# Grouping a layer's column-tiled products in the order of TensorE, and loading a layer's constants through GpSimd

## The chip, the cores and the metric

The kernel runs on one NeuronCore of one Trainium2 chip. The number that counts is the device time of one execution in microseconds; before the change it is 3792.88 us, the median of three runs that lie between 3792.59 and 3792.96 us. TensorE (PE) does the matrix products, VectorE (DVE), ScalarE (ACT) and GpSimd (POOL) the elementwise work, and SyncE (SP) mostly issues transfers (DMAs). Each engine carries out its own queue in order and waits for others by semaphores.

## The reference

32 graphs of 512 nodes, with 256 features per node (x) and a 512x512 0/1 matrix (adj), go through four layers. Each layer is x + layer(relu(layernorm(x))).

- Layer 0 is graph attention with 4 heads of 64 features: h = x W, scores leaky_relu(src_i + dst_j) where adj is set, softmax over j, product with h, elu.
- Layer 1 is graph attention with one head and 256 features, with the softmax over i in place of j.
- Layer 2 has scores leaky_relu((h * a_0) h^T); where adj is 1 they are used, the rest is masked; softmax over j, product with h.
- Layer 3 is a transformer block: queries, keys and values (Wqkv), 8 heads of 32 features, masked softmax, output product (Wo), layernorm, a hidden layer of 1024 features with relu (W1, W2), layernorm.

```
scores = einsum('bhqd,bhkd->bhqk', q * scale, k)
attn   = softmax(where(allowed, scores, -inf))
ctx    = einsum('bhqk,bhkd->bhqd', attn, v)
x      = layernorm(x + ctx @ Wo.T + bo)
x      = layernorm(x + relu(x @ W1.T + b1) @ W2.T + b2)
```

## The kernel before

`quick_path` handles one graph at a time with 128 partitions by NT = 4 tiles of 128 nodes and KD = 2 tiles of 128 features. Everything is float32; the masks are bfloat16. An f32 product appears as two MATMUL instructions in the profile, so the counts there are twice those in the code (transposes by an identity matrix count once).

**Jobs and places.** The layers don't issue instructions; they hand jobs to a `Plan` (`plan.dve`, `plan.act`, `plan.dma`, `plan.matmuls`). The job number `at` of graph `number` gets the place `number * ROUND + PLACES[at]`, with ROUND = 100000 and one table of 509 numbers, `PLACES`, that is the same for all graphs. `carry_out` sorts all jobs by place and issues them in that order, chaining the jobs of one engine to each other, so that each engine's queue is exactly that order. The last number of the table is 506629: about five graphs are in work at a time, each in another stage, and after the first graphs every stretch of 100000 places, a round, holds one whole graph's worth of jobs from several graphs. A matmul job is a list of products that stand together in PE's queue. Costs such as `takes`, `fixed`, `FULL`, `HALF` were for the making of the table and do nothing at run time.

**Buffers.** A `Kind` is a tag with a number of slots: two PSUM slots `ps_a`, two `ps_b`, one `ps_ct`, one `ps_to`; in SBUF six `p`, two `p3`, eight `st` and so on.

**Products.** PE's jobs are of three kinds. Most use the whole array (128 rows by 128 columns). In layer 3, `ps_s`, the scores of four heads, are four products with 32 contracted rows each, one per quarter of the rows (32*128 in the profile). `ps_ct`, values times probabilities, and `ps_to`, the sums of the probabilities by a matrix of ones, are four products with 32 output columns each, one per quarter of the columns (128*32). Per graph there are 8 jobs of each of the three, in the loop over `g` (2 groups of heads) and `j` (4 tiles of keys); each is 8 MATMULs. `ps_ct` and `ps_to` are separate jobs with separate places, so other products can stand between them.

```
plan.matmuls(0.93, *((ps_ct[at], v[...], p[:, r], ...) for r, at in enumerate(heads)))
plan.matmuls(0.98, *((ps_to[at], ones, p[:, r], ...) for r, at in enumerate(heads)))
```

Between the scores and these, ACT takes the exponential (two instructions into `p3`) and DVE multiplies by the mask m3.

**Layer 1's column sums.** For each j, DVE makes p (`scalar_tensor_tensor` of rows and mc), then ACT copies p into mc only to accumulate its sum (`activation`, AF.Copy, accum_out=rt[:, 3]), which adds an accumulator read; then DVE takes the reciprocal and ACT scales wh with it.

**The start.** Before the plan, the preamble loads the weights and constants of all layers through ACT's queue (`weight_of`, `rows_of`, `cols_of`), 6 for layers 0 to 2 and 15 for layer 3, in program order ahead of ACT's first computation. DVE folds the attention vectors into w0_t and w1_t (lines 396 to 405), scales bqk_c (407), and a small product ps_bv (line 414) folds the values' bias into bo_r. SP loads adj and x of graph 0 (places 0 and 38476). Layer 0 needs the transposed mask mT: four DMA transposes on SP, then the source scores go through DRAM to all partitions (rows_d, rows).

**Helpers' lines.** Line 208 stands for all DVE and ACT jobs, 242 for products, 240 for transposes, 229 for SP's DMAs.

## Time and profile before

| | us |
|---|---|
| median of three runs | 3792.88 |
| the profiled execution | 3795.71 |
| its span, first to last instruction | 3794.3 |
| PE busy | 3675.7 (97%) |
| DVE busy | 2726.3 (72%) |
| ACT busy | 1899.4 (50%) |
| POOL busy | 0.9 |
| mean granted TensorE clock | 0.981 of full |

The profile gives busy time by engine, the span in 40 slices, waits by releaser, groups of instructions by shape, and a timeline in which neighbouring instructions of one group are merged (start, length, xcount). A product's length is modelled and overlaps the next one's; the time that a group holds PE is the distance from its start to the next start.

### The profile page before, as it was taken

What the parts mean: (1) busy time and instruction counts of PE and PEld (TensorE: products, weight loads), DVE (VectorE), ACT (ScalarE), POOL (GpSimd) and SP (SyncE); (2) the same over time, 40 slices, a digit from 0 to 9 for tenths busy, and PEclk for the clock granted to TensorE, in tenths of its full rate; (3) what the DMA queues carried; (4) which work ended last, traced back from release to release, by engine and by line L of the source; (5) the groups of instructions that cost most, each with busy time, mean ns of one, the idle gap of its engine ahead of it and who ended that gap; (6) DMA issues with size and microseconds to landing.
All of it is one profiled execution on the core that took longest, in us unless ns stands there. A gap on an engine that the chain in (4) does not pass through costs nothing.

```text
span 3794.3 us, 51918 instructions
## 1 busy us (share of the span) xinstructions
PE 3675.7 (97%) x19974; PEld 2333.5 (62%) x19974; DVE 2726.3 (72%) x6139; ACT 1899.4 (50%) x3649; POOL 0.9 (0%) x10
## 2 busy tenths in 40 slices
PE   4799999999999999999999999999999999999996
PEld 4656666665666665666666666656666656566543
DVE  4677777787777787777787777777777778777653
ACT  1255544555544555545555554455555455554543
POOL 0000000000000000000000000000000000000000
PEclk7799999999999999999999999999999999999998
DMA  3211111111101111101111101111111111110000
GB/s 115 61 43 43 35 31 43 48 43 43 44 22 44 47 43 43 45 21 48 43 43 49 40 21 48 43 43 48 42 29 37 43 48 44 43 34 15 15 9 10
DMA packets 156239, 152.74 MB, mean 40 GB/s; under 512 B 90064, under 2 KB 126416, under 8 KB 151888
## 3 DMA queue, kind: packets, MB, share of 16 engines
q1 hardware_dynamic: 149632, 144.35, 12.4%
q10 hardware_dynamic: 6352, 4.99, 0.4%
q8 instruction: 160, 2.62, 0.3%
q14 instruction: 95, 0.78, 0.1%
HBM read 114.57 MB, written 17.96 MB: 35 GB/s over the span
## 4 chain that ended last, share of the span: by engine, by line
PE 95%; DVE 2%; DMA 1%; ACT 1%; issue 0%; ACTq 0%; DVEq 0%
PE ps_o L242 25%; PE ps_f L242 24%; PE ps_s L242 7%; PE ps_wh L242 6%; PE ps_ct L242 6%; PE ps_to L242 6%; PE ps_qk L242 6%; PE ps_t L240 4%; PE ps_e L242 4%; PE ps_v L242 3%; PE ps_wo L242 3%; DVE p L208 1%; PE ps_y L240 1%; DMA rows<-rows_d 0%; DMA ff_t<-in_L_gnn_W_dram 0%; PE ps_sp L240 0%
## 5 line engine op out<-in xcount | busy, mean ns | idle before, releaser
L242 PEld LDWEIGHTS ps_o<-wh,p 128*128 128x128 f32 x5120 | 694.8, 196 | 171.5 <-issue 93.6
L242 PE MATMUL ps_o<-wh,p 128*128 128x65 f32 (+1 forms) x5120 | 749.7, 301 | 21.6 <-DVE p L208 21.5
L208 DVE TENSOR_TENSOR p<-p,m 128x2048 f32<-128x2048 f32 x256 | 585.1, 2286 | 47.2 <-ACT p L208 47.2
L208 ACT ACTIVATE p<-ps_s 128x1024 f32<-128x1024 f32 x512 | 500.7, 1021 | 177.5 <-PE ps_s L242 177.5
L242 PE MATMUL ps_f<-tT,ff_t 128*128 128x512 f32 x1024 | 464.4, 602 | 1.7 <-ACT tT L208 1.7
L242 PE MATMUL ps_f<-ff_t,f 128*128 128x256 f32 x2048 | 459.2, 380 | 0.0
L242 PEld LDWEIGHTS ps_f<-ff_t,f 128*128 128x128 f32 x2048 | 384.5, 190 | 64.7 <-issue 16.7
L208 DVE SCALAR_TENSOR_TENSOR p<-rows,rt,mT 128x512 f32<-128x512 f32 x512 | 366.9, 738 | 14.0 <-DMA rows<-rows_d 14.0
L242 PEld LDWEIGHTS ps_f<-tT,ff_t 128*128 128x128 f32 x1024 | 191.5, 192 | 219.2 <-issue 171.8
L208 ACT ACTIVATE f<-ps_f,ff1b_c 128x512 f32<-128x512 f32 x256 | 165.6, 685 | 311.4 <-PE ps_f L242 311.4
L208 ACT ACTIVATE h<-x,shift,rstd 128x256 f32<-128x256 f32 x512 | 272.3, 590 | 86.8 <-PE ps_o L242 46.7
L242 PE MATMUL ps_s<-qk 32*128 32x512 f32 x2048 | 296.2, 641 | 1.2 <-ACT p L208 1.1
L242 PE MATMUL ps_ct<-p,v 128*32 128x512 f32 x2048 | 272.8, 605 | 5.0 <-DVE p L208 4.9
L242 PE MATMUL ps_to<-p,ones 128*32 128x512 f32 x2048 | 266.3, 603 | 3.0 <-DVE p L208 3.0
L242 PE MATMUL ps_o<-h,p 128*128 128x257 f32 x1024 | 246.6, 388 | 0.4 <-DVE p L208 0.4
L242 PE MATMUL ps_qk<-h3T,wqkv_t 128*128 128x512 f32 x512 | 233.1, 599 | 1.5 <-ACT h3T L208 1.5
L242 PEld LDWEIGHTS ps_o<-h,p 128*128 128x128 f32 x1024 | 186.6, 190 | 77.5 <-DVE inv L208 26.0
L208 DVE BATCH_NORM_STATS2 st<-x 128x6 f32<-128x256 f32 x512 | 204.5, 415 | 2.2
L208 DVE COPY spr<-ps_sp 8x128 f32<-8x128 f32 (+1 forms) x64 | 17.8, 278 | 258.8 <-PE ps_sp L240 258.8
L208 ACT ACTIVATE mc<-p 128x512 f32<-128x512 f32 x128 | 80.5, 629 | 209.8 <-DVE p L208 209.8
L240 PEld LDWEIGHTS ps_t<-ident,h 128*128 128x128 f32 x1024 | 125.3, 146 | 95.7 <-issue 27.2
L242 PEld LDWEIGHTS ps_s<-qk 32*128 32x128 f32 x2048 | 82.0, 183 | 163.9 <-issue 50.2
(120 smaller groups left out, 4488.6 us busy)
## 6 DMA issues: line engine op xcount, KB each, us to landing
adj<-in_adj_dram SPq DMA_DIRECT2D x32, 1024.0 KB
rows<-rows_d SPq DMA_DIRECT2D x32, 1024.0 KB
x<-in_x_dram SPq DMA_DIRECT2D x32, 512.0 KB
rows<-rows_d SPq DMA_DIRECT2D x32, 512.0 KB
out_dram<-y SPq DMA_DIRECT2D x32, 512.0 KB
inv<-in_d SPq DMA_DIRECT2D x32, 256.0 KB
ff_t<-in_L_gnn_W_dram ACTq DMA_DIRECT2D x2, 1024.0 KB
mT<-m SPq DMA_TRANSPOSE x128
```

Of the source, the lines that this page charges most:

```text
L208: return [getattr(unit, method)(*map(real, args), **{k: real(v) for k, v in kw.items()})]
L240: made.append(self.nc.tensor.transpose(*map(real, c)))
L242: made.append(self.nc.tensor.matmul(*map(real, c[:3]), start=c[3], stop=c[4]))
```

## The change

1. `ps_ct` and `ps_to` of one (g, j) become one matmul job: four value products, then four sums.
2. In layer 1 ACT's copy for the sum is removed; DVE's `scalar_tensor_tensor` that makes p gets accum_out=rt[:, 3].
3. Layer 3's 15 loads leave ACT's queue. They become POOL DMAs, planned just behind graph 0's loads of x and adj (place 19808), each waiting until graph 0's x has landed. The folding that needs them (bqk_c, ps_bv, bo_r, b2_r, b1_r: six DVE jobs and one PE job) becomes jobs at place 150000, in all queues between graph 0's layer 0 and graph 1's.
4. A new table of 497 numbers (12 jobs fewer), ending at 491710. x now comes before adj. `st` has 7 slots in place of 8; ff2b_r gets its own buffer; ACT's table is loaded by another call at the same spot. The `takes` numbers change too, which does nothing at run time.

```
-                plan.matmuls(
-                    0.93,
+                plan.matmuls(
+                    1.764,
                     *(
                         (ps_ct[at], v[:, j, g * P + r * HD : g * P + (r + 1) * HD], p[:, r], j == 0, j == NT - 1)
                         for r, at in enumerate(heads)
                     ),
+                    *((ps_to[at], ones, p[:, r], j == 0, j == NT - 1) for r, at in enumerate(heads)),
                 )
-                plan.matmuls(0.98, *((ps_to[at], ones, p[:, r], j == 0, j == NT - 1) for r, at in enumerate(heads)))
...
             plan.dve(
-                "scalar_tensor_tensor", p[:, j], rows[:, 0], rt[:, 2, j : j + 1], mc, OP.max, OP.mult, fixed=0.21
+                "scalar_tensor_tensor", p[:, j], rows[:, 0], rt[:, 2, j : j + 1], mc, OP.max, OP.mult,
+                accum_out=rt[:, 3, j : j + 1], fixed=0.21,
             )
-            plan.act("activation", mc, p[:, j], AF.Copy, accum_out=rt[:, 3, j : j + 1], fixed=0.4)
...
+    def load(self, tile, source, behind):
+        wait = mybir.DependencyInfo(mybir.DependencyClass.Sync, mybir.DependencyReason.DATA)
+        def call():
+            made = self.nc.gpsimd.dma_start(tile, source)
+            self.tc.add_manual_dep(made.ins, behind().made.name, wait, reason="in turn")
+            return [made]
+        return self.put("POOL", 1.0, 0.1, [], [], call)
...
-    wqkv_t = weight_of(nc, const, wqkvT, "wqkv_t")
+    wqkv_t = weight_of(nc, const, wqkvT, "wqkv_t", load=later)
...
+    plan.aside(max(PLACES[:2]) + 1)
+    for tile_, source in late:
+        plan.load(tile_, source, lambda: first)
+    plan.aside(ROUND + ROUND // 2)
+    plan.dve("tensor_scalar_mul", bqk_c[:, :KD], bqk_c[:, :KD], SCALE)
+    bv_w, ps = new("p", "bv_w", [P, N]), new("ps_a", "ps_bv", [P, N])
+    for k in range(KD):
+        plan.dve("tensor_copy", bv_w[:, cut(k, P)], bv_c[:, k : k + 1].to_broadcast([P, P]))
+    plan.matmuls(HALF, *((ps[:, :D], bv_w[:, cut(k, P)], wo_t[:, k], k == 0, k == KD - 1) for k in range(KD)))
+    plan.dve("tensor_add", bo_r, ps[:, :D], bo_r)
+    plan.dve("tensor_scalar_add", b2_r, b2_r, -2.0)
+    plan.dve("tensor_add", b1_r, b1_r, ff2b_r)
...
 PLACES = [
-    0, 38476, 64990, 78041, 65188, 65188, 65188, 72767, 130287, 255105, 157691, 242001, 270048, 276929, 44320,
...
+    19807, 0, 43241, 57619, 64598, 73580, 81389, 88138, 134062, 235662, 143142, 287307, 285553, 232853, 15635,
...
```

Sorted by place, the two tables put PE's jobs of one round in these orders. Written from the first `ps_s` of a graph to the products that follow its attention; names as in the profile, the number is the count of jobs, c+t is the new joint job, and ps_o is of layer 0 (o0), 1 (o1) or 2 (o2).

```
before: s, 2 o1, s, 2 wh, to, ct, s, 2 wh, ct, 2 wh, to, s, sp, to, 8 t, ct, s, 3 e, to, e,
        ct, s, ct, 3 y, 2 e, to, s, 2 y, 2 e, ct, to, 2 o0, s, 2 o0, 2 o2, y, ct, o2, 2 to,
        2 o2, ct, 3 o0, then t, wo, wh, o0, f1, f2, qk, v
after:  s, 2 o1, s, 2 wh, c+t, s, 4 wh, c+t, s, c+t, sp, 8 t, s, 4 e, c+t, s, 3 y, 2 e, c+t,
        s, e, 2 y, e, c+t, s, y, 4 o0, 2 o2, c+t, c+t, 2 o2, then wo, o0, t, wh, f1, f2, v, qk
```

On SP, graph 0's order is x, adj, mT, mT, rows_d, mT, rows, mT (before: adj, x, four mT, rows_d, rows), and likewise for every graph.

## The prediction

> **What bounds the kernel now.** I read the page's busy shares first, then the waits of PE, then busy time by stretch, then one round of the timeline.

> ```profile
> PE 3675.7 (97%) x19974; PEld 2333.5 (62%) x19974; DVE 2726.3 (72%) x6139; ACT 1899.4 (50%) x3649; POOL 0.9 (0%) x10
> ```

> ```profile
> 0.00:100.00 100.00, 46.67 (x185) 39.91 (x185) 41.28 (x109) 15.45 (x38) 0.86 (x10) 0.73 0.41 128
> 100.00:200.00 100.00, 80.66 (x426) 67.26 (x425) 61.77 (x171) 31.04 (x79) 0.00 (x0) 0.79 0.14 39
> 300.00:400.00 100.00, 100.00 (x582) 64.76 (x580) 79.23 (x175) 53.10 (x103) 0.00 (x0) 1.00 0.15 46
> 3400.00:3500.00 100.00, 100.00 (x548) 64.25 (x547) 71.20 (x161) 48.42 (x94) 0.00 (x0) 1.00 0.10 30
> 3700.00:3794.00 94.00, 64.47 (x306) 30.35 (x306) 37.12 (x55) 28.74 (x41) 0.00 (x0) 0.84 0.03 10
> ```

> The columns are PE, PEld, DVE, ACT, POOL, then clock and DMA. From 300 to 3500 us PE is busy without a break, and the list of waits for that stretch is empty. Only the ends, where few graphs are in work, have idle PE. So DVE, ACT and DMA work is free in the middle, unless an order makes PE wait for it; what counts is how long PE's own products take.

> They don't take the same time everywhere. One round in PE's timeline:

> ```profile
> 2017.57 5.31 PE L242 MATMUL ps_qk<-h3T,wqkv_t 128*128 128x512 f32 x12
> ...
> 2028.77 1.05 PE L242 MATMUL ps_wh<-w_t,h0T 128*128 128x264 f32 x4
> 2029.65 3.62 PE L242 MATMUL ps_o<-wh,p 128*128 128x256 f32 x16
> ...
> 2038.99 1.16 PE L242 MATMUL ps_wh<-w_t,h0T 128*128 128x264 f32 x4
> 2040.08 1.07 PE L242 MATMUL ps_to<-p,ones 128*32 128x512 f32 x8
> 2040.96 1.04 PE L242 MATMUL ps_ct<-p,v 128*32 128x512 f32 x8
> 2041.94 1.14 PE L242 MATMUL ps_s<-qk 32*128 32x512 f32 x8
> ...
> 2044.09 1.06 PE L242 MATMUL ps_ct<-p,v 128*32 128x512 f32 x8
> 2045.09 1.16 PE L242 MATMUL ps_wh<-w_t,h0T 128*128 128x264 f32 x4
> 2046.18 1.07 PE L242 MATMUL ps_to<-p,ones 128*32 128x512 f32 x8
> ...
> 2130.59 0.59 PE L242 MATMUL ps_qk<-h3T,wqkv_t 128*128 128x512 f32 x1
> ```

> From ps_qk to the next graph's is 113.02 us: the round. From start to next start, eight ps_to followed by ps_ct, the same shape of tile, hold PE 0.88 us, but eight ps_ct followed by ps_wh 1.00. Four ps_wh hold it 0.88 between full products, but 1.09 between ps_s and ps_to. No engine is waited for there: changing the tile shape costs PE about 0.1 us at each edge. That is the term the change acts on.

> **The change part by part.**

> *The joint job and the new order.* In a round of the old order the column-tiled products (ct, to) are left 13 times for another shape (8 for full products, 5 for ps_s) and follow one of their own 3 times. In the new order they are left 7 times and follow their own 9 times. ps_s is entered and left as often as before. Three rows price that.
> - Leaving: 0.996 against 0.883 us (0.972 where the one before was column-tiled too). Old, by place: 15.53 us for the 16 jobs. New: 7 x 0.972 + 9 x 0.883 = 14.75. Gain 0.78.
> - Entering from a full product: 12 times before, 6 after, 0.093 each (1.09 above is 0.88 plus one such edge plus the next). Gain 0.56.
> - The first full product behind another shape: 0.05 (small ones) to 0.105 us (wh, e) dearer; 15 such before, 9 after, but two dear ps_e are new among them. Item by item, gain 0.21.

> Sum 1.54 us a round: 113.03 becomes 111.49. The same listing over all 32 graphs, the incomplete rounds at both ends included, gives 3611.7 us of full-clock PE work before and 3564.8 after: 46.9 less, near 28 full rounds (322 to 3487 us) x 1.54 = 43.1 and 3.8 at the ends. The remaining 182.6 us of the span are the start, the end and the slow clock there.

> That holds if PE waits as little as now. DVE's work per round (2726 / 32 = 85 us) and ACT's (59) stay well below 111. But individual products stand close to their inputs. A sums job of the old order and the mask product that it uses:

> ```profile
> 2045.84 2.29 DVE L208 TENSOR_TENSOR p<-p,m 128x2048 f32<-128x2048 f32 x1 [0.35 <-ACT p L208]
> ...
> 2048.45 0.16 PEld L242 LDWEIGHTS ps_to<-p,ones 128*32 128x32 f32 x8
> ```

> Its data is there at 2048.13, 0.32 us ahead. For each product I added up, in either order, the PE time since the product that its inputs descend from, less the durations of the DVE and ACT steps between: its room if nothing queues in front of those steps. The pair shown has 1.84 us by this count, so queues took 1.52; at another one (mask product 2061.52 + 2.28, ct at 2064.22) they took 1.2 of 1.64. In the new order no room is negative. The smallest are ps_f1 behind the transposes of n (0.88 us for a chain of 0.84), ps_e behind its transposes (1.45 for 1.30), and ct behind ps_s 1.30, 1.55 and 2.22 us. The old order, with 0.05 and 0.3 as its smallest, doesn't wait. I take no wait; if queues take 1.52 of the 1.30, the wait is 0.2 a round, and two or three such places make the 0.5 us a round (31 rounds: 16 us) that the range takes in.

> *The sum on DVE.* ACT loses 4 x (0.629 + 0.189) us a round, hidden: ACT is idle 50%. On DVE, p takes

> ```profile
> L208 DVE SCALAR_TENSOR_TENSOR p<-rows,rt,mc 128x512 f32<-128x512 f32 x128 | 94.3, 738 | 0.0
> L208 ACT ACTIVATION_READ_ACCUMULATOR mc<-p 128x1 f32 x128 | 24.2, 189 | 0.0
> ```

> No accumulating DVE instruction is in the trace. Lower bound 0, upper bound an extra read of 0.189 us plus the whole p again, 0.74: 0 to 3.7 us a round. I take the read alone, as ACT pays only that beside its pass: 0.76 us of DVE. PE hides it (85 of 111 us busy); without that cover the loss is 24 us in all. The chain to ps_o of layer 1 gets shorter by ACT's 0.63.

> [...]

> *The start.* ACT's first computation stands behind the 15 issues:

> ```profile
> 16.19 0.23 DVE L208 BATCH_NORM_AGGREGATE mv<-st 128x2 f32<-128x6 f32 x2
> 22.50 0.59 ACTq L37 DMA_DIRECT2D ff2b_r<-in_L_gnn_b_dram  x1
> 23.20 0.30 ACT L208 ACTIVATE rstd<-mv,eps 128x4 f32<-128x4 f32 x1 [21.17 <-DMA g_r<-in_L_gnn_ln_g_dram]
> ```

> Its input is ready at 16.42, so the first chain can move 6.8 us forward; x first in SP's queue may add to that, up to 11 in all, when DVE's folding of w0 and w1 (ends 19.0) becomes the last. Two things give some back. SP now has rows_d, which waits for the scores, ahead of two of the four mT transposes (1.3 us each, 5.23 for four): one more transpose is in the path, 1.3 us. And the folding at place 150000 stands between graph 0's layer 0 and graph 1's first transposes: 0.17 + 2 x 0.36 on DVE, 2.08 for ps_bv on PE, about 3 us, with graph 1's copy of h0T queued behind it on DVE. Net -2.5 us, from -11 to +8.

> *The loads on POOL.* The folding is reached about when graph 0's layer 0 ends, near 80 us (x is written at 79.4 to 80.6). ACT issues the 15 in 7.41 to 23.09, 15.7 us. No POOL DMA is in the trace. Bounds: as on ACT, or each as long as ACT's longest, 2.40: 36 us. From x's landing at 12 at the latest they'd be issued by 28 to 48, and landed some 11 us later (the longest DMA in the chain is 11.3). Both are before 80, so I take 0; each microsecond past 80 would stop DVE's queue and with it PE, 1 for 1. They also share the DMA engines with mT and rows of graph 0: 1 MB of rows took 41.88 - 37.01 = 4.9 us; up to 5 us more, in the range.

> [...]

> *The end.* The last graph's reciprocals now wait for sums that stand behind the values' products: +0.9 us.

> Sum: -46.9 - 2.5 + 0.9 = -48.5. The profiled execution of 3795.71 would become 3747.2, and the median, which lies 2.8 below it, 3744.4; I say 3744.

> **The rivals.**

> *A. DVE's accumulation makes it slower.* If p costs the full 0.93 us more and PE waits for all of it, that is 3.7 us a round over 31 rounds: +115, with -48.5 about 3859. It decides from 1.6 us of wait a round up (48.5 / 31). For it: DVE's multiplies end just ahead of their products. Against it: DVE idles 26 us a round, and layer 1's chain loses an ACT step.

> *B. The order is too tight.* PE waits 0.5 to 1.2 us a round for ACT or DVE: 16 to 37 us lost, 3760 to 3781. For it: the 0.04 us of room of ps_f1 and queues I didn't cost. Against: the old order is as tight and PE doesn't wait.

> *C. The loads come late.* At 5 us each on POOL they'd end near 12 + 75 + 11 = 98: +18, 3762. Slower than before only from 7 us each (48.5 us late: 128.5 - 23, by 15).

> *D. It changes nothing.* It would need the shape costs to be something else, say a slow weight load, that moves with the jobs. The 0.88 and 1.00 us of the same eight products speak against it: 3790.

> **How the numbers follow.** Forecast 0.74, 3728 to 3762: the start's -11 to +8, waits up to 0.3 us a round, and some 7 us less for the idle time of the first three rounds, whose order changes too and which I priced only at its two ends. B 0.11; C 0.04; A 0.09, of which 0.07 end above and 0.01 level; D 0.02. The range takes in the forecast, C and half of B: 3728 to 3772. A difference under 0.2% (7.6 us) can't be told from no change here. Faster: forecast, B, C and the rest of A, 0.90. Same 0.03, slower 0.07.

> **What would show it.** A round of 111.5 us from ps_qk to ps_qk with no PE wait between 300 and 3500; c+t jobs of 1.86 us (0.88 + 0.98) where another shape follows. The first rstd near 16 us. p's mean in layer 1 at 0.74 and a read below 0.2. POOL's last DMA before 60 us. A round near 113 without waits would refute the shape costs; a wait of PE by DVE p or ACT tT would be rival A or B; a gap of PE near 75 us that ends by a DMA would be C.

## The result, and the profile after

The changed kernel takes 3757.43 us (median of 4, 3756.09 to 3758.1) against 3792.92 for the kernel before, run beside it: ratio 0.9905, 95% interval [0.9888, 0.9923]. That is 35.5 us less; 48.5 were forecast. The profiled span went from 3794.25 to 3756.16 us, 38.1 less, and the comparison below goes by these two.

The page of the changed kernel, busy time of PE and the rest:

```profile
PE 3635.0 (97%) x19974; PEld 2366.4 (63%) x19974; DVE 2732.6 (73%) x6267; ACT 1803.8 (48%) x3393; POOL 11.1 (0%) x25
```

The same stretches as before, with the same columns (PE, PEld, DVE, ACT, POOL, granted clock, DMA share, GB/s):

```profile
0.00:100.00 100.00, 48.29 (x194) 41.72 (x195) 42.77 (x110) 15.27 (x38) 11.12 (x25) 0.70 0.44 129
100.00:200.00 100.00, 77.59 (x309) 64.78 (x309) 49.67 (x137) 23.16 (x56) 0.00 (x0) 0.62 0.13 37
300.00:400.00 100.00, 100.00 (x543) 61.60 (x543) 75.28 (x169) 52.97 (x99) 0.00 (x0) 1.00 0.16 41
3400.00:3500.00 100.00, 98.56 (x547) 62.28 (x540) 69.09 (x157) 48.77 (x85) 0.00 (x0) 1.00 0.04 12
3700.00:3756.00 56.00, 34.96 (x117) 21.87 (x115) 14.77 (x42) 11.66 (x22) 0.00 (x0) 0.82 0.03 11
```

The middle is again full: the list of PE's waits between 340 and 3450 us is empty. The second row is the surprise. From 100 to 200 us PE did less than before (309 matrix instructions where there were 426) at a granted clock of 0.62 where it had been 0.79.

One round of PE's timeline, from the first ps_v to the next graph's, with one of the joint units:

```profile
2006.62 0.59 PE L259 MATMUL ps_v<-wqkv_t,h3T 128*128 128x256 f32 x2
...
2029.14 1.07 PE L259 MATMUL ps_ct<-p,v 128*32 128x512 f32 x8
2030.03 1.04 PE L259 MATMUL ps_to<-p,ones 128*32 128x512 f32 x8
2031.00 1.14 PE L259 MATMUL ps_s<-qk 32*128 32x512 f32 x8
...
2118.00 0.59 PE L259 MATMUL ps_v<-wqkv_t,h3T 128*128 128x256 f32 x2
```

The round is 111.38 us, and 111.37 or 111.38 almost throughout (before: 113.02 or 113.03). In the unit shown, ps_ct followed by ps_to holds PE 0.89 us from start to start, and ps_to followed by ps_s 0.97.

Layer 1's p with its accumulation, and the read that it costs (count, total us, mean ns, idle before):

```profile
L214 DVE SCALAR_TENSOR_TENSOR p<-rows,rt,mc 128x512 f32<-128x512 f32 x128 | 93.5, 749 | 2.3
L214 DVE DVE_READ_ACCUMULATOR p<-rows,rt,mc 128x1 f32 x128 | 10.6, 83 | 0.0
```

The start, with the first and the last of POOL's loads:

```profile
5.90 0.85 POOL L243 DMA_DIRECT2D wqkv_t<-in_L_gnn_Wqkv_dram  x1 [4.46 <-DMA x<-in_x_dram]
7.61 0.30 ACT L214 ACTIVATE rstd<-mv,eps 128x4 f32<-128x4 f32 x1 [5.57 <-DVE mv L214]
24.24 0.55 POOL L243 DMA_DIRECT2D ff2b_r<-in_L_gnn_b_dram  x1
```

**Where the 38.1 us came from.** I cut both spans where graph 1 and graph 29 begin layer 3 (its first ps_qk or ps_v) and split PE's time in each end into three: its work at full clock, what a clock of 0.5 adds to it (half of PE's busy time in the stretches where the granted clock is 0.5), and idle time. The 28 rounds between have no idle time and no slow clock. (What the half clock adds is therefore an estimate from the busy time; layer 0's four ps_o ahead of a ps_wh hold PE 1.60 us at 120.6 us of the changed kernel, where the clock is 0.50, and 0.84 at 2078.6, where it is 1.00.)

| us | before | after | difference |
|---|---|---|---|
| head, to graph 1's layer 3 | 322.12 | 335.96 | +13.8 |
| - work at full clock | 209.4 | 205.9 | -3.5 |
| - added by the half clock | 35.7 | 51.4 | +15.7 |
| - idle | 77.0 | 78.7 | +1.7 |
| 28 rounds | 3164.8 | 3118.6 | -46.2 |
| tail, from graph 29's layer 3 | 307.3 | 301.7 | -5.7 |
| - work at full clock | 253.7 | 250.0 | -3.7 |
| - added by the half clock | 12.0 | 9.2 | -2.9 |
| - idle | 41.6 | 42.5 | +0.8 |

PE's work fell by 53.4 us, more than the 46.9 of the forecast. What was lost is in the head: it should have become shorter and became 13.8 us longer, by about as much as the half clock added. The clock's record begins only at 32.2 us before and at 22.0 after; ahead of that it counts as full, though eight ps_t take 2.01 us at 14.8 us of the changed kernel and 1.04 in the middle. PE's busy time there is 7.3 and 6.8 us, so the differences in the table would change by some 0.3 us.

When graph 0 and graph 1 pass through the head, the difference after minus before develops like this: first ps_t -12.2 us, graph 0's first ps_o -9.2, graph 1's first ps_o -3.5, graph 0's first ps_e +10.4, its layer 3 +19.4. The early start was there; 8.7 of its 12.2 us were used up by graph 1's first ps_o (at 96 us), and the rest by graph 0's layer 1 (its ps_sp at 131.3 us, 124.9 before).

Two views of 3.4 us stretches show the clock in that place, with PE's busy time in the second column and the clock in the third from the end. Before:

```profile
114.20:117.60 3.40, 3.40 (x13) 2.73 (x14) 2.46 (x7) 0.59 (x1) 0.00 (x0) 0.50 0.00 0
117.60:121.00 3.40, 3.40 (x28) 3.26 (x27) 1.78 (x4) 0.75 (x2) 0.00 (x0) 1.00 0.00 0
```

After:

```profile
117.20:120.70 3.50, 3.50 (x14) 3.13 (x13) 0.27 (x1) 0.37 (x1) 0.00 (x0) 0.50 0.00 0
120.70:124.10 3.40, 3.40 (x16) 3.21 (x15) 0.00 (x0) 0.37 (x1) 0.00 (x0) 0.50 0.00 0
124.10:127.50 3.40, 3.40 (x16) 3.21 (x16) 0.75 (x3) 0.00 (x0) 0.00 (x0) 0.50 0.00 0
...
151.80:155.20 3.40, 3.30 (x8) 2.71 (x9) 0.46 (x3) 2.77 (x4) 0.00 (x0) 0.51 0.22 43
155.20:158.60 3.40, 3.40 (x18) 2.95 (x17) 0.42 (x1) 0.72 (x3) 0.00 (x0) 1.00 0.00 0
```

In both, PE has something to do for all but 0.1 us of these stretches. Before, the clock comes back at 117.6; after, it stays at 0.5 until 155.2, though PE is busy from 117.2 to 127.5 without a break. Half clock lasted 102 us in the head before, with 71 us of PE's busy time in it, and 147 us after, with 103. The last section comes back to this busy PE at half clock.

### The profile page after: what moved, and what is told of

Its sections match the earlier page's. It is cut to its first block, busy times and chain, and to the rows that moved or that the text cites. A ratio compares the mean times of both kernels' runs of the same rounds, so it can differ in the third digit from the quotient of the medians.

```text
span 3756.2 us, 51774 instructions
## 1 busy us (share of the span) xinstructions
PE 3635.0 (97%) x19974; PEld 2366.4 (63%) x19974; DVE 2732.6 (73%) x6267; ACT 1803.8 (48%) x3393; POOL 11.1 (0%) x25
## 3 DMA queue, kind: packets, MB, share of 16 engines
q1 hardware_dynamic: 149632, 144.35, 13.8%
q10 hardware_dynamic: 1248, 1.05, 0.1%
## 4 chain that ended last, share of the span: by engine, by line
PE 95%; DVE 3%; ACT 1%; DMA 1%; issue 1%; SPq 0%; ACTq 0%; DVEq 0%
PE ps_o L259 25%; PE ps_f L259 24%; PE ps_s L259 7%; PE ps_ct L259 7%; PE ps_wh L259 6%; PE ps_qk L259 6%; PE ps_to L259 6%; PE ps_e L259 4%; PE ps_t L257 4%; PE ps_v L259 3%; PE ps_wo L259 3%; DVE p L214 1%; PE ps_y L257 1%; DVE st L214 0%; DMA mT<-m 0%
## 5 line engine op out<-in xcount | busy, mean ns | idle before, releaser
L259 PE MATMUL ps_o<-wh,p 128*128 128x65 f32 (+1 forms) x5120 | 750.5, 303 | 30.2 <-DVE p L214 24.6
L259 PEld LDWEIGHTS ps_o<-wh,p 128*128 128x128 f32 x5120 | 705.6, 200 | 102.7 <-issue 60.5
L259 PE MATMUL ps_o<-h,p 128*128 128x257 f32 x1024 | 239.0, 385 | 0.0
L214 DVE BATCH_NORM_STATS2 st<-x 128x6 f32<-128x256 f32 x512 | 195.6, 415 | 6.8 <-DMA x<-in_x_dram 4.7
L214 ACT ACTIVATE rstd<-mv,eps 128x4 f32<-128x4 f32 x192 | 56.4, 294 | 298.6 <-DVE mv L214 286.0
L257 PE MATMUL ps_t<-ident,h 128*128 128x128 f32 x1024 | 172.6, 281 | 25.0 <-ACT h L214 17.6
L259 PEld LDWEIGHTS ps_s<-qk 32*128 32x128 f32 x2048 | 81.3, 182 | 164.6 <-ACT y L214 78.0
```

What stands on the lines that cost most here:

```text
L214: return [getattr(unit, method)(*map(real, args), **{k: real(v) for k, v in kw.items()})]
L257: made.append(self.nc.tensor.transpose(*map(real, c)))
L259: made.append(self.nc.tensor.matmul(*map(real, c[:3]), start=c[3], stop=c[4]))
```

## The experiments

Theory T: the head lost its time to the granted clock, which the new order lets fall earlier and come back later. Rival L: the head is a chain of DVE and ACT steps and PE's clock matters little. Rival F: the loads through GpSimd and the folding between the graphs hold it up. For the rounds: theory S, the price of changing the tile shape, against O, something else in the new order.

### The unit alone, in the old order (joint_only)

```diff
                 plan.matmuls(
-                    0.93,
+                    1.764,
                     *((ps_ct[at], v[...], p[:, r], j == 0, j == NT - 1) for r, at in enumerate(heads)),
+                    *((ps_to[at], ones, p[:, r], j == 0, j == NT - 1) for r, at in enumerate(heads)),
                 )
-                plan.matmuls(0.98, *((ps_to[at], ones, p[:, r], j == 0, j == NT - 1) for r, at in enumerate(heads)))
 PLACES: the old list; a unit takes the later of its two old places (two units: that of ps_to)
```

> The old kernel, in which each values' job and its sums' job are put as one unit of eight products, at the later of their two old places (at the sums' place where a reader of both stands before the values' place); all else, the order of everything else included, is the old kernel's. Theory S (what a round gained is the price of changing the tile shape): the listing of this order has 9 column-tiled units followed by their own kind, 4 that go to ps_s and 3 to full products (old: 3, 6 and 8), and by the prediction's rows a round of 111.64 us, 1.4 less than 113.03; the whole 42 us less, about 3751, with the head unchanged, first layer 3 of graph 1 at 320 to 323 us. Rival O (the new order of the other work made the gain): the round stays at 112.8 to 113.1 and the time above 3785.

Measured: 3793.77 us, ratio 0.9999 [0.9989, 1.0008], and a round of 113.03, as in the kernel before to a hundredth. By the time alone rival O has won. The list of PE's waits between 500 and 3400 us says otherwise (us in total, times, longest):

```profile
PE ps_t L240 <- DVE mv L208: 11.6, 25, 0.5
PE ps_o L242 <- DVE p L208: 9.6, 25, 0.4
```

The kernel before has no wait there. This one waits twice in each round, 0.85 us, and PE's busy time in a round is 112.18 where it was 113.03: the unit saves 0.85 us of work, and 0.85 us of new waits take it back. The same rows that promised 1.39 us a round were therefore too dear by some 0.5 in this order. The timeline shows the first wait:

```profile
2047.94 0.28 PE L240 MATMUL ps_sp<-ident,rt 128*16 128x128 f32 x1
...
2048.26 0.28 DVE L208 COPY spr<-ps_sp 16x128 f32<-16x128 f32 x1
2048.46 0.16 DVE L208 BATCH_NORM_AGGREGATE mv<-st 128x2 f32<-128x6 f32 x1
...
2048.68 1.06 PE L240 MATMUL ps_t<-ident,h 128*128 128x128 f32 x8 [0.46 <-DVE mv L208]
```

And the kernel before at the same place:

```profile
2048.24 0.28 PE L240 MATMUL ps_sp<-ident,rt 128*16 128x128 f32 x1
2048.45 1.07 PE L242 MATMUL ps_to<-p,ones 128*32 128x512 f32 x8
2049.45 1.09 PE L240 MATMUL ps_t<-ident,h 128*128 128x128 f32 x8
```

In the old order a job of eight ps_to (1.00 us from start to next start) stood between ps_sp and these transposes, and covered DVE's two steps. Joined to its ps_ct it stands elsewhere. The other wait is the same with a ps_ct between the last ps_y and ps_o2. That the two sums agree to a hundredth of a us I take for chance: each wait is set by the DVE steps beside it.

### The unit, with the two covers back (joint_cover)

```diff
 PLACES of joint_only, but the units 337/338 and 369/370 take the earlier of their two old places
-    399642 -> 396426 (ps_ct, ps_to between ps_sp and ps_t)
+    428748 -> 425188 (ps_ct, ps_to between ps_y and ps_o2)
```

> Like joint_only, but two of the eight units stand at the earlier of their two old places: so a column-tiled unit lies again between ps_sp and the transposes behind it, and another between the last ps_y and ps_o2, the two places where joint_only made PE wait 0.5 and 0.4 us a round. If joint_only's gain was eaten by these two uncovered DVE steps alone: no PE wait in the middle, and by the prediction's rows (8 units followed by their own kind, 3 by ps_s, 5 by full products) a round of 112.07 us, 0.95 less than before, about 3764. If the rows are wrong and the unit gains nothing in itself: 112.8 to 113.1 again, 3790 or more.

Measured: 3771.78 us, ratio 0.9941 [0.9925, 0.9958]; a round of 112.21, no PE wait between 500 and 3400 us. So the unit is worth 0.82 us a round by itself (forecast from the rows: 0.95), and S stands: with the old order otherwise kept, nothing but the changes of shape has gone. The other half of the changed kernel's 1.65 us needs the new places.

### The loads back on ACT's queue (loads_back)

```diff
-    wqkv_t = weight_of(nc, const, wqkvT, "wqkv_t", load=later)
+    wqkv_t = weight_of(nc, const, wqkvT, "wqkv_t")
...
-    plan.aside(max(PLACES[:2]) + 1)
-    for tile_, source in late:
-        plan.load(tile_, source, lambda: first)
-    plan.aside(ROUND + ROUND // 2)
-    plan.dve("tensor_scalar_mul", bqk_c[:, :KD], bqk_c[:, :KD], SCALE)
...
+    nc.vector.tensor_scalar_mul(bqk_c[:, :KD], bqk_c[:, :KD], SCALE)
...
```

> The changed kernel with layer 3's constants loaded on ACT's queue again and folded ahead of the first graph, as before; order, units and the sum on DVE stay new. If the loads through GpSimd, with the folding between the graphs, give what graph 1's first products showed (3.5 us earlier than before): 3 to 8 us slower than the changed kernel, 3760 to 3765. Rival F (the folding inside the order is what held the head up, 13.8 us): 3743 to 3750. In both cases the round stays at 111.37.

Measured: 3761.86 us (0.9919 [0.9902, 0.9935]), round 111.38, layer 3 of graph 1 at 338.9 us: 4.4 us slower than the changed kernel, 3.0 of it in the head. The loads help; F falls. Its start is that of the kernel before (graph 0's first ps_o at 45.6 us, 44.0 before), and its head is 16.8 us longer, 1.6 of them there already at that ps_o. The other 15 or so are left for the new order; head_old_a and head_old_b, below, test that.

### Idle products in the waits (after_warm, before_warm)

```diff
+    warm = new("ps_ct", "warm", [P, N])
+    for place, count in ((80715, 11), (132759, 3), (140000, 8), (180715, 10), (240000, 6), (254300, 3), (257400, 3)):
+        plan.aside(place)
+        for _ in range(count):
+            plan.matmuls(FULL, (warm, ident, wqkv_t[:, 0, :N], True, True))
```

In the kernel before: `((95439, 10), (152147, 7), (195439, 10), (252147, 11))`, and the method `aside` with it.

> The changed kernel with 44 idle products (identity by 512 columns of a weight, into the values' PSUM tile, read by nobody) where PE waits in the first 155 us: 11 behind the first ps_sp, 3 and 8 inside and behind graph 0's layer 0, 10 behind graph 1's ps_sp, 6, 3 and 3 behind graph 1's layer 0. Theory T (the head is long because TensorE's granted clock stays at half for 147 us, with 103 us of PE work in it): the clock stays at 1.0 for most of the head, the first layer 3 of graph 1 comes at 305 to 322 us in place of 336, and the time falls by 14 to 30 us to 3727 to 3743. Rival L (the head is a chain of DVE and ACT steps, and PE's clock doesn't matter): the clock rises, but the time stays within 4 us of 3757, or grows by what the idle products run over.

> The old kernel with 38 such idle products in its waits of the first 140 us (10 behind the first ps_sp, 7 behind graph 0's layer 0, 10 and 11 for graph 1). It had 103 us of half clock with 72 us of PE work in it. Theory T: 8 to 20 us faster than before, 3773 to 3785, and the changed kernel with idle products is 43 to 55 us ahead of this one, more than the 35.5 without them, since the changed kernel lost some 15 us more to the clock. Rival L: both unchanged, the distance stays at 35.5.

| | time, us | half clock in the head, us | added by it | idle and idle products | layer 3 of graph 1 at |
|---|---|---|---|---|---|
| before | 3792.9 | 102 | 35.7 | 77.0 | 322.1 |
| before_warm | 3785.83, 0.9979 [0.9970, 0.9989] | 58 | 24.6 | 81.3 | 315.7 |
| after | 3757.4 | 147 | 51.4 | 78.7 | 336.0 |
| after_warm | 3746.76, 0.9878 [0.9862, 0.9895] | 65 | 28.1 | 84.6 | 320.1 |

Both heads become shorter by products whose result nobody reads, so the clock costs time and L falls. But T predicted too much in both: 14 to 30 us for after_warm, where the median gained 10.7, and 3773 to 3785 us for before_warm, which came to 3785.83. In after_warm's profile the clock's share fell by 23.3 us and idle time grew by 5.9: part of what PE does faster it then waits for DVE and ACT.

How much of the 13.8 us between the two heads is the clock's, these runs leave open. By the medians the two warmed kernels are 39.1 us apart (forecast by T: 43 to 55, by L: 35.5), only 3.6 more than without the idle products. In the profiles the warmed heads are 4.5 us apart, which would leave 9.3 to the clock; in those 4.5 us the half clock still adds 3.5 more than in before_warm, and idle time 3.3, less 2.3 of work. But the profiled execution of after_warm is the fastest of its four (3741.92 us) and that of before_warm the slowest of its ten (3789.76), which can make the two heads look nearer than they are as a rule. What is shown of the clock's part lies between 3.6 and 9.3 us, and the idle products left 58 and 65 us of half clock in place.

### The old order in the head (head_old_a, head_old_b)

```diff
+HEAD = [ ... the old places, for a unit the later of its two (of two units: that of ps_to) ... ]
+UNTIL = 273000          # head_old_b: 373000
...
-        place = self.number * ROUND + self.table[self.at] if self.place is None else self.place
+        if self.place is None:
+            place, head = self.number * ROUND + self.table[self.at], self.number * ROUND + HEAD[self.at]
+            place = head if head < UNTIL else place + 1 if place >= UNTIL else UNTIL + place * 1e-7
+        else:
+            place = self.place
...
-    plan.aside(max(PLACES[:2]) + 1)
+    plan.aside(max(HEAD[:2]) + 1)
...
-    plan.aside(ROUND + ROUND // 2)
+    plan.aside(153000)
```

The old order brings adj ahead of x again, and the loads on GpSimd and the folding get places that fit it.

> The changed kernel with the old order for everything whose old place is below 273000 (the first graph up to layer 1's scores, the second through layer 0, the third up to its first transposes), and the new order from there; constants still on GpSimd, the folding behind graph 0's layer 0. If the changed kernel's head is long because of its order (with the constants and the start as in the changed kernel, it lost 17.2 us to joint_only's head up to graph 1's layer 3): layer 3 of graph 1 at 316 to 328 us in place of 336, rounds of 111.4, time 3738 to 3750. If the constants on GpSimd, the folding or the sum on DVE are what holds the head up: 332 to 338 us, 3752 to 3760.

> The same with the border at 373000, one round later, so that the head up to graph 0's layer 3 is in the old order. If the loss arises evenly over the head (it grew from -10.7 us at graph 1's first products to +6.2 at graph 0's layer 3 between the two kernels with idle products): layer 3 of graph 0 at 196 to 206 us in place of 222, graph 1's at 314 to 324, time 3733 to 3746, some 5 us ahead of head_old_a. If only the first stage matters: the same as head_old_a within 2 us.

Measured: head_old_a 3745.13 us, 0.9872 [0.9852, 0.9891], graph 1's layer 3 at 322.0; head_old_b 3738.05, 0.9853 [0.9837, 0.9870], layer 3 of graph 0 at 201.5 and of graph 1 at 315.2, rounds of 111.37. (One of head_old_a's four executions took 9352 us at a mean granted clock of 0.516; the median counts it, the ratio leaves it out, and nothing here shows why.) With the head's order put back (head_old_b) the changed kernel gains 19 us; its head is then 20.8 us shorter, of which 17.3 are the half clock's (34.1 where it was 51.4) and 5.6 idle time, less 2.1 of work. The view by stretches, to be held against the second row of the changed kernel's:

```profile
0.00:100.00 100.00, 49.37 (x199) 42.91 (x199) 42.14 (x112) 15.45 (x38) 11.68 (x25) 0.70 0.44 129
100.00:200.00 100.00, 80.55 (x418) 66.27 (x418) 60.94 (x174) 29.92 (x74) 0.00 (x0) 0.81 0.13 43
```

From 100 to 200 us the clock is 0.81 and PE does 418 instructions (0.62 and 309). head_old_b is 7 us ahead of head_old_a: the loss arises along the head, as expected, not at its first stage alone. So the order is what made the head long: the loads and the sum on DVE are the same in these kernels. That the order does it through the clock is what the split of PE's time says, and the idle products confirm it for a part.

### Both, as the best version (head_old_warm)

head_old_b with idle products at `((95438, 11), (153001, 8), (195438, 10), (252146, 11))`.

> head_old_b with 40 idle products in the four long waits of its head (11 and 10 behind the first two ps_sp, 8 and 11 behind the first two graphs' layer 0). Its head is 208 us of PE work, 34 of slow clock and 73 of idle. In the old kernel such products took 11 us off the slow clock's share and the head became 6.5 us shorter. Theory T in the form the runs leave it (the clock is a cost of its own, of which waits for DVE and ACT give back about a third): 5 to 9 us below head_old_b, 3729 to 3733. If the rest of that head is DVE's and ACT's alone: 3736 to 3740.

Measured: 3730.57 us, 0.9832 [0.9815, 0.9848]: faster than both kernels, 62.7 us below the one before and 26.9 below the changed one. The half clock adds 24.6 us (34.1 in head_old_b), idle time with the idle products grows from 73.1 to 76.8, layer 3 of graph 1 begins at 307.7. The gain of 7.5 us lies where the corrected theory had it (5 to 9).

```profile
0.00:100.00 100.00, 71.16 (x277) 51.15 (x277) 43.51 (x117) 15.32 (x39) 11.68 (x25) 0.85 0.42 129
100.00:200.00 100.00, 88.49 (x431) 65.84 (x432) 67.64 (x187) 33.84 (x80) 0.00 (x0) 0.88 0.13 43
```

PE's busy time is larger by the idle products; what counts is that ACT and DVE got further by 200 us than in head_old_b (33.8 and 67.6 us of work in the second stretch against 29.9 and 60.9).

### Transposes as idle work (before_warm_t)

```diff
-        for _ in range(count):
-            plan.matmuls(FULL, (warm, ident, wqkv_t[:, 0, :N], True, True))
+        for _ in range(8 * count):
+            plan.matmuls(0.11, (warm[:, :P], wqkv_t[:, 0, :P], ident))
```

> before_warm with each idle product (0.86 us) replaced by eight idle transposes of 128 columns (0.11 us each), so the same time of PE. If transposes hold the clock as products do: 50 to 70 us of half clock in the head and layer 3 of graph 1 at 314 to 319 us, as with products (58 us, 315.7). If they don't: the clock falls some 4 us into each group, about 100 us of half clock as without any (102), the transposes then take twice as long and run over the waits, and layer 3 of graph 1 comes at 330 us or later.

Measured in a single execution: half clock for 51 us, layer 3 of graph 1 at 314.7, 3788.8 us. Transposes hold the clock as well as products do: it is 1.00 from 36.6 to 45.7 us, where PE does nothing else.

### DVE's accumulation alone (sum_only)

```diff
                 "scalar_tensor_tensor", p[:, j], rows[:, 0], rt[:, 2, j : j + 1], mc, OP.max, OP.mult,
+                accum_out=rt[:, 3, j : j + 1], fixed=0.21,
             )
-            plan.act("activation", mc, p[:, j], AF.Copy, accum_out=rt[:, 3, j : j + 1], fixed=0.4)
```

> The old kernel with layer 1's sum taken by DVE's accumulation alone, ACT's copy left out, old order and units. If the accumulation costs a read of 0.1 us (83 ns by the changed kernel's trace) and nothing of the pass: the round stays at 113.03, DVE's work per round grows by 0.4 us and ACT's falls by 3, layer 3 of graph 1 comes 0 to 3 us earlier. If the pass took half rate in this order: p at 1.48 us, and PE waits for p in layer 1.

Measured in a single execution: round 113.03, layer 3 of graph 1 at 320.3 us (322.1), 3794.7 us. p takes 737 ns (738 without accumulation), and beside it stands

```profile
L208 DVE DVE_READ_ACCUMULATOR p<-rows,rt,mc 128x1 f32 x128 | 10.3, 80 | 0.0
```

DVE's busy time in 113 us is 84.76 (84.75), ACT's 56.54 (59.20). The busy time didn't grow by the 0.4 us that I expected: in the timeline each read begins 0.07 us ahead of the end of its pass, so nearly all of its 0.08 us was counted as busy already. This part neither gains nor costs anything by itself.

## Why the prediction was right and wrong

**The joint unit and the order: right, and a little too small.** The prediction had 1.54 us a round: 0.78 for leaving the column-tiled jobs, 0.56 for entering them and 0.21 for the full product behind another shape. Measured: 1.65. The jobs of ct and to take 14.70 us a round (15.52 before): 0.82. The other 0.82 is on the products beside them, ps_o -0.29 and ps_o2 -0.20 the most, and -0.09 each at ps_wh, ps_sp, ps_e and ps_y, with ps_t +0.09. The two later terms together, 0.77, were 0.05 too small. Over the rounds 46.2 us against 43.1, and at the two ends 7.2 of work against 3.8.

**"I take no wait": right.** The list of PE's waits in the middle is empty. joint_only shows what this was worth: the same unit without suitable places waits 0.85 us a round and gains nothing. So "the change of shape" was only half of the cause. In joint_only the rows were too dear as well (0.85 us of work where they said 1.39), so that the sum in the new order comes out within 0.11 us is in part luck. I had priced edges as if they could be taken out one at a time; a job that is moved also stops covering the latency of the DVE step that it stood beside.

**The sum on DVE: right that it is hidden, wrong in size.** I took 0.189 us for the read, as ACT's; it is 0.083. The pass itself takes 749 ns in the changed kernel and 737 in sum_only, against 738 without the accumulator, far from the upper bound (the whole p again, 1.48 us).

**The start: the term was right, and it went elsewhere.** The -6.8 for the constants' issues on ACT's queue shows in head_old_b: its first ps_sp is at 27.87 us against 34.95, 7.1 earlier. In the changed kernel x comes earlier as well, and the first rstd is at 7.61, not near 16. The two things that give some back came as priced: from ps_sp to ps_o graph 0 takes 10.2 us (9.1 before; 1.3 was taken for the transpose behind rows), and from layer 0's last ps_o to graph 1's first ps_t, with the folding between, 9.1 us (6.6 before; 3 was taken). The loads were issued by 24.8, far from the 80 us where they'd have hurt. The item as a whole shows in loads_back: without it 4.4 us are lost by the medians, 3.0 of them in the head, where 2.5 were forecast. Yet of the lead of 12.2 us at graph 0's transposes nothing was left at layer 1.

**The step that failed** is a sentence, not a term: "The remaining 182.6 us of the span are the start, the end and the slow clock there." I subtracted from the full-clock work and left this rest as it was, apart from the start's own steps. It isn't constant. The order sets when PE works densely, and the granted clock changed with it: half clock lasted 102 us in the head of the old order and 147 in that of the new one. At half clock the same work takes longer: by the table's split, +15.7 us in the head and -2.9 in the tail. (That the order lengthened the head is shown by head_old_b; that all of it went by way of the clock is not, see the idle products.) I had allowed "some 7 us less" for the idle time of the first rounds and nothing for the clock, neither as a term nor as a rival, though the profile of before showed 0.73 and 0.79 in its first two rows. With 53.4 us of work gained, 12.8 lost to the clock and 2.5 to idle time, 38.1 remain. That the forecast missed by no more than 13 us is partly luck, since 6.5 us more of work than forecast made up for half of what the clock took. It is luck, too, that the time lies in the stated range: the room at its upper end was meant for a late start, waits in the rounds and late loads, none of which came.

**The end:** +0.9 us was forecast for the last reciprocals, and the tail's idle time grew by 0.8; that it is these reciprocals was not tested.

**The rivals.** A falls with the 749 ns. B falls with the empty list of waits, C with the 24.8 us. D falls with joint_cover. A loss in the head was not among the rivals.

## What to carry to other kernels

A job's place in an order is worth two things: the edges that it makes and the latency that it covers; when it is moved, price both, and look for the DVE or ACT step that stood in its shadow. An order that suits the steady rounds can lose in the ramp part of what it gains there (13.8 of 46.2 us here), so the ramp may deserve an order of its own, and products that nobody reads, put where PE waits anyway, can hold its clock up (58 us of half clock in the head where it was 102, 65 where it was 147), though PE then waits more for DVE and ACT (in after_warm the clock's share fell by 23.3 us and idle time grew by 5.9). A sum of PE work at full clock needs a term for the granted clock wherever the clock's row is below 1.0.
